# Two convolution layers on one core: x1's stores, the first small maps, layer 1's constants and the inner convolution rearranged

## The chip, the cores and the metric

The kernel runs on one core of a Trainium2 chip, in float32 throughout. The core has five engines that work through their own instruction lists in order and wait for each other through semaphores: TensorE (PE in the profile, with PEld for its weight loads), VectorE (DVE), ScalarE (ACT), GpSimd (POOL) and SyncE (SP), which here only issues DMA transfers. ScalarE issues transfers too. The metric is the device time of one execution in microseconds, lower is better.

## The reference

Input x is (8, 256, 64, 64). Two layers, each added to its own input, each preceded by a group normalisation `_gn` over 32 groups of 8 channels:

```python
# layer 0: an involution-like block; the 3x3 weights are computed from the input
x1 = conv1x1(x, w1, b1)                  # 32 channels
x2 = conv1x1(x, w2, b2)                  # 32 channels, unfolded 3x3 with reflect padding
x3 = conv1x1(x, w3, b3)                  # 256 channels, unfolded 3x3 with zero padding
h = relu(bn1(concat([x1, unfold3(x2)]))) # 320 channels
h = relu(bn2(conv1x1(h, cw1)))           # 32 channels: "the inner convolution"
w = conv1x1(h, cw2, cb2)                 # 32 groups x 9 taps
out = einsum("bgskhw,bgkhw->bgshw", unfold3(x3), w)
x = x + out
...
# layer 1: 7x7 local attention (4 heads of 64 channels) beside a dynamic 3x3 branch
att = softmax(einsum("bdn,bdkn->bnk", q, unfold7(k) + unfold7(pe)))
out_att = einsum("bnk,bdkn->bdn", att, unfold7(v))
wts = softmax(Wfc @ x, over the 9 taps)
out_conv = sum over taps of dwconv(relu(dwconv(x, w1)), w2) * wts
x = x + rate1 * out_att + rate2 * out_conv
```

## The kernel before

An image is cut into 8 bands of 8 rows (512 pixels), so there are 64 bands. One loop runs over g, from -12 to 63. In round g layer 1 works on band g, and layer 0 on the bands ahead of it: the small maps and value maps of band g + 12, the hidden maps of g + 11, the tap products of g + 10. Rounds -12 to -1 hold layer 0 alone (`alone`); from round 0 on both layers share the engines. From round 52 on layer 0 has nothing left.

A round has 8 steps, a step 6 positions. The order of each engine's instructions is written out by hand (`tc.manual_schedule()`): `beside` lists the work of a step at its head, middle and end, `steer` its loads, and `after(n, f)` puts f off by n positions. Calls of one position run in the order in which they were put off. The engines then wait only for data and for buffers: each tile has a tag with `bufs` slots, and a tile's writer waits for the readers of the tile that had its slot.

Layer 0 of one band, with the names that the change touches:

- `small_maps` (L332) makes x1 and x2 (64 channels) on TensorE, two half-bands of 4 rows stacked in one PSUM tile `small`. `write_maps` (L347, L351) adds the bias and writes them, three shifted copies of x2 and one of x1 for each half, eight ScalarE instructions. GpSimd then copies the edges (L357 to L366).
- `value_maps` (L375, L380, L382) makes x3 in two halves of 128 channels, `x3n`, and stores each to DRAM. In rounds of layer 0 alone ScalarE issues these stores. `values_by_group` (L396 to L404) reads them back in another layout, `x3q`.
- `hidden_maps` (L424) applies bn1 and relu in three instructions, `hid`, and TensorE does the inner convolution in 4 + 4 + 4 matmuls (L434). When layer 0 is alone all go to one PSUM tile and the second relu (L441) follows. Otherwise `one` does the first 8 in step 4 and ScalarE copies the sum out (L446); `two` does the last 4 in step 6, VectorE adds the copy (L450), and the relu follows.
- `tap_weights` makes the tap weights on TensorE (L470). VectorE multiplies each of the 9 with the shifted x3 (L483, `prod`, two slots). When layer 0 is alone TensorE sums three of the nine (L504) and VectorE adds that sum (L511, `combine`); all other products GpSimd adds to `xg`, which begins as x (L491). `take` reads the statistics for layer 1's normalisation (L519); `keep` then stores the finished x1 of the layer (`x<-xg`, four transfers, L529).

`x_tile` "xs" feeds the statistics of layer 0's normalisation some 9 bands ahead (`first_stats`, L287), and `scaled_weights` (L300, L301, L308) folds the normalisation into an image's weights; when the 8th band of an image's x1 is done, `norm_rows` computes layer 1's scale and bias. `load_rows`, `normalise` (L572), `values` (L601, L608) and `store_values` (L621, L625) then prepare layer 1's first bands.

The constants are loaded by `load`, all issued by ScalarE (L110). Those marked `now=False` (`c2`, the tap weights' matrix; `wq`, `wk`, `wv`, `wfc`, `mask` of layer 1) are put off and issued by `layer1_loads`, right before the first round. That also subtracts the ninth tap's column from `wfc` (`difference`, L205, two VectorE instructions), in rounds -10 and -9 of layer 0 alone, and scales `wv` (L200).

In layer 1, `branch_weights` (L886) is the largest matmul group, its exponentials go through ScalarE (L891), and `dynamic_sum` divides: GpSimd adds two sums (L899), limits the total (L902), VectorE takes reciprocals in two halves (L907), GpSimd multiplies (L908) and weighs the depthwise result `oc` (L912, L913), which ScalarE wrote in `depthwise_end` (L879). `oc` has two slots.

Of the kernel before, what the change touches and what calls it, by code (L numbers as in the profile page):

```python
# [10 lines left out]
F32 = mybir.dt.float32  # L11
# [7 lines left out]
P = 128  # L19
C = 256  # L20
# [67 lines left out]
def conv_layers_kernel(ctx: ExitStack, tc: tile.TileContext, ins: dict, out: bass.AP):  # L88
# [16 lines left out]

    late = []

    def load(name, shape, src=None, now=True):
        t = const.tile(shape, F32, name=f"c_{name}")
        late.append(lambda: nc.scalar.dma_start(out=t, in_=ins[name] if src is None else src))  # L110
        if now:
            late.pop()()
        return t
# [10 lines left out]
    gc = load("gc", [P, NCT, P])  # L124
    c2 = load("c2", [P, KK, P], now=False)
    wq = load("wq", [P, NCT, C], ins["wq"].rearrange("(t p) n -> p t n", p=P), now=False)
    wk = load("wk", [P, NCT, C], ins["wk"].rearrange("(t p) n -> p t n", p=P), now=False)
    wv = load("wv", [P, NCT, C], ins["wv"].rearrange("(t p) n -> p t n", p=P), now=False)
    wfc_in = ins["wfc"].rearrange("(t p) k n -> p t k n", p=P)
    wfc = load("wfc", [P, NCT, KK - 1, C], wfc_in[:, :, : KK - 1], now=False)  # L130

# [59 lines left out]
    def layer1_loads():  # L191


        last = w1.tile([P, NCT, 1, C], F32, tag="oc", name="last")
        for f in late:
            f()
        nc.scalar.dma_start(out=last, in_=wfc_in[:, :, KK - 1 :])

        def first():
            nc.vector.tensor_scalar(wv, wv, rate1, None, ALU.mult)  # L200

        def difference(kt):
            nc.vector.tensor_sub(wfc[:, kt], wfc[:, kt], last[:, kt].to_broadcast([P, KK - 1, C]))  # L205

        return [first, lambda: difference(0), lambda: difference(1)]

# [131 lines left out]
    def write_maps(b, i, p12, half):  # L340
        im = images[b]
        t, bias = im.x2[i], im.bias
        for u in half:
            r, o = u * R // 2, 64 * u
            for q, (dst, src) in enumerate(((1, 0), (0, 0), (0, 1))):
                n = W - (q != 1)
                nc.scalar.activation(  # L347
                    t[32 * q : 32 * q + 32, r + 1 : r + 1 + R // 2, dst : dst + n],
                    p12[o : o + 32, :, src : src + n], AF.Identity, bias=bias[o : o + 32, 0:1],
                )  # L350
            nc.scalar.activation(  # L351
                t[96:128, r : r + R // 2, :], p12[o + 32 : o + 64], AF.Identity, bias=bias[o + 32 : o + 64, 0:1]
            )
        if half[-1] == 0:
# [58 lines left out]
    def hidden_maps(b, i, alone):  # L413
# [7 lines left out]
        def hidden(t):  # L421
            n = P if t == 0 else 96
            hid = w0.tile([P, R, W], F32, tag="hid", name=f"hid_{b}_{i}_{t}", bufs=2)
            nc.scalar.activation(  # L424
                hid[:n], im.x2[i][:n, t : t + R, :], AF.Relu, bias=bn1b[:n, t : t + 1], scale=bn1s[:n, t : t + 1]
            )
            hids.append(hid)
# [14 lines left out]

        def one(home):
            ph = conv(home, 0, 2, 0, 1)
            after(1, lambda: hidden(2))
            after(2, lambda: nc.scalar.copy(h2, ph))  # L446

        def two(home):
            ph = conv(home, 2, 3, 2, 2)
            after(1, lambda: nc.vector.tensor_add(h2, ph, h2))  # L450
            after(3, lambda: relu(h2))

        hidden(0)
        after(3 if alone else 5, lambda: hidden(1))
        if alone:
# [4 lines left out]
            after(12, lambda: after(4, lambda ph=conv(home, 2, 3, 0, 2): relu(ph)))  # L460
        return [two, one]

    def tap_weights(b, i, u, alone, at):
# [49 lines left out]
        def take():  # L513
# [7 lines left out]
            if alone:  # L521
                after(9, lambda: keep(nc.scalar))
            else:
                keep(nc.sync)

        def keep(queue):
            for q in range(NQR):
                v = im.xg[i][q * REL : (q + 1) * REL].rearrange("p s r c -> p s (r c)")
                queue.dma_start(out=pieces(im.x1[i], q), in_=v)  # L529
# [346 lines left out]
    def depthwise_end(b, i, ct, acc):  # L876

        oc = w1.tile([P, BAND], F32, tag="oc", name=f"oc_{b}_{i}_{ct}")
        nc.scalar.activation(oc, acc.rearrange("p r c -> p (r c)"), AF.Copy, scale=rate2)  # L879
# [13 lines left out]
    def dynamic_sum(b, i, ct, ex, oc):  # L893
# [7 lines left out]

        engine.tensor_scalar(tot, tot, 1.0, 1.0e37, ALU.add, ALU.min)  # L902
        rec = w1.tile([P, BAND // 2], F32, tag="rec", name=f"rec_{b}_{i}_{ct}", bufs=1)
# [17 lines left out]

        after(9, lambda: quotient(0))
        after(13, lambda: quotient(1))
        after(15, weigh)


    def beside(g, s):
# [73 lines left out]
    def steer(g, s):  # L1001
# [22 lines left out]
    with tc.manual_schedule():  # L1024
# [15 lines left out]
        for _ in range(32):  # L1040
            advance()
        for n, f in enumerate(layer1_loads()):
            after(4 * STEPS * (3 + n), f)

        pending, before, conv, convs, maps = [], None, None, [], []
        for g in range(-AHEAD, B * NB):
            b, i = divmod(g, NB)
            for s in range(STEPS):
# [5 lines left out]
                if g >= 0:  # L1054
                    nm = f"{b}_{i}_{ct}_{m}"
                    weighted = []
                    if m % 2 == 0:
# [154 lines left out]
```

## Time and profile before

| what | value |
| --- | --- |
| time, median of 3 runs | 3856.01 us (3853.47 to 3856.48) |
| the profiled execution's own time | 3854.63 us |
| its span | 3852.8 us |
| mean granted TensorE clock | 0.994 |
| busy: PE / DVE / POOL / ACT | 97% / 89% / 81% / 73% |
| DMA | 490.14 MB, mean 127 GB/s |
| first matmul of `branch_weights` (L886) | at 235.5 us |

The profile is one execution. Its page gives the busy time of each engine, the span in 40 slices, the chain of work that ended last, and the costliest groups of instructions. The trace behind it answers finer questions: what an engine did in order of time in some stretch, and for what it waited. In an answer in order of time a line gives the start, the duration, the engine (SPq and ACTq are transfers being issued), the line of the kernel, the operation, its output and inputs, and in brackets how long the engine had been idle and who released it.

### The profile page before, as it was taken

The numbers are of one execution on the slowest core, as the hardware profiler recorded it, in microseconds if no ns is written. First come the engines' busy times: TensorE is split into PE (matmuls) and PEld (weight loads), VectorE is DVE, ScalarE is ACT, GpSimd is POOL, SyncE is SP. The second block draws the span as 40 slices with busy tenths as digits, with TensorE's granted clock in tenths as the row PEclk, the third lists the DMA queues.
The fourth block names the chain that finished last, engine by engine and source line by source line (L and its number), as shares of the span: only waits on it lengthen the run. The fifth ranks groups of instructions, "written<-read, shape, count | busy, mean of one in ns | idle before, by whom it ended". The sixth has DMA issues, their size and how long they took to land.

```text
span 3852.8 us, 71646 instructions
## 1 busy us (share of the span) xinstructions
PE 3756.3 (97%) x24620; PEld 2109.9 (55%) x24620; DVE 3434.4 (89%) x7125; ACT 2809.2 (73%) x6770; POOL 3116.8 (81%) x2100
## 2 busy tenths in 40 slices
PE   6889999999999999999999999999999999999998
PEld 3445555555555555555555555555555555555554
DVE  6879999999999999899998999999999899978877
ACT  4457777777777777777777777777777777677776
POOL 4868888888897888888888888888888888855565
PEclk9999999999999999999999999999999999999999
DMA  8764544544444544544544544454544544232221
GB/s 247 210 177 128 142 118 129 151 126 118 133 135 131 145 123 115 148 135 127 136 116 142 142 125 120 126 149 125 136 115 117 138 119 114 74 97 78 79 67 37
DMA packets 438926, 490.14 MB, mean 127 GB/s; under 512 B 62016, under 2 KB 324256, under 8 KB 438304
## 3 DMA queue, kind: packets, MB, share of 16 engines
q1 hardware_dynamic: 421984, 469.79, 44.1%
q10 hardware_dynamic: 16576, 15.76, 1.3%
q8 instruction: 194, 3.18, 0.4%
q14 instruction: 172, 1.41, 0.1%
HBM read 343.76 MB, written 145.10 MB: 127 GB/s over the span
## 4 chain that ended last, share of the span: by engine, by line
PE 81%; POOL 10%; DVE 3%; DMA 2%; ACT 2%; issue 2%; SPq 1%; ACTq 0%; POOLq 0%; DVEq 0%
PE pf L886 39%; PE small L799 6%; PE ptp L787 6%; POOL xg L491 6%; PE pk L706 5%; PE pq L684 5%; PE sco L750 5%; PE p L375 5%; PE pv L601 5%; PE pw L470 2%; POOL ex L1106 2%; PE small L332 1%; DVE prod L483 1%; PE small L434 1%; DMA x<-x3n 1%
## 5 line engine op out<-in xcount | busy, mean ns | idle before, releaser
L886 PE MATMUL pf<-yp,c_wfc 128*128 128x512 f32 x4096 | 1916.8, 594 | 11.3 <-DVE prod L483 6.3
L491 POOL TENSOR_TENSOR xg<-xg,prod 128x1024 f32<-128x1024 f32 x549 | 1199.8, 2185 | 132.5 <-DVE prod L483 103.6
L886 PEld LDWEIGHTS pf<-yp,c_wfc 128*128 128x128 f32 x4096 | 739.6, 190 | 711.4 <-issue 654.7
L1106 POOL TENSOR_TENSOR ex<-ex,ex 128x1024 f32<-128x1024 f32 x384 | 908.8, 2367 | 68.5 <-ACT ex L891 65.0
L891 ACT ACTIVATE ex<-pf 128x512 f32<-128x512 f32 x1024 | 604.0, 590 | 347.9 <-PE pf L886 269.2
L843 DVE SCALAR_TENSOR_TENSOR acc<-yp,c_chan,acc 128x504 f32<-128x504 f32 (+3 forms) x1104 | 775.5, 702 | 63.2 <-ACT acc L834 42.8
L483 DVE SCALAR_TENSOR_TENSOR prod<-pw,c_par,x3q 128x1040 f32<-128x1040 f32 x576 | 732.7, 1294 | 107.9 <-PE pw L470 60.8
L869 DVE SCALAR_TENSOR_TENSOR acc<-hid,c_chan,acc 128x504 f32<-128x504 f32 (+3 forms) x1024 | 751.1, 733 | 18.1
L781 ACT ACTIVATE prob<-prob,tot 128x196 f32<-128x196 f32 x1024 | 412.9, 452 | 242.4 <-DVE tot L779 236.8
L772 ACT ACTIVATE prob<-prob,nmax 128x196 f32<-128x196 f32 x1024 | 458.2, 450 | 101.3 <-DVE nmax L764 101.2
L907 DVE RECIPROCAL rec<-tot 128x256 f32<-128x256 f32 x256 | 445.7, 1741 | 28.3 <-POOL tot L902 27.5
L789 ACT COPY pt<-ptp 112x512 f32<-112x512 f32 x511 | 295.9, 579 | 111.8 <-PE ptp L787 111.8
L764 DVE CUSTOM_DVE_ANT_0 prob<-sco,c_mask 128x196 f32<-128x196 f32 x1024 | 324.8, 355 | 31.0 <-PE sco L750 31.0
L787 PEld LDWEIGHTS ptp<-ident,prob 128*112 128x112 f32 x2044 | 227.3, 133 | 184.4 <-issue 132.7
L787 PE MATMUL ptp<-ident,prob 128*112 128x128 f32 x2044 | 319.5, 279 | 0.0
L908 POOL TENSOR_TENSOR tot<-tot,rec 128x256 f32<-128x256 f32 x254 | 185.8, 732 | 145.7 <-DVE rec L907 139.7
L799 PEld LDWEIGHTS small<-pt,vt 112*64 112x64 f32 x8144 | 258.6, 138 | 79.8 <-issue 60.5
L799 PE MATMUL small<-pt,vt 112*64 112x64 f32 x8144 | 294.2, 225 | 3.3 <-DMA vt<-vd 1.8
L601 PE MATMUL pv<-c_wv,yp 128*128 128x256 f32 x1056 | 253.5, 383 | 1.8 <-ACT yp L572 1.8
L902 POOL TENSOR_SCALAR tot<-tot 128x512 f32<-128x512 f32 x127 | 243.9, 1920 | 11.1
L470 PEld LDWEIGHTS pw<-h2n,c_c 128*128 128x128 f32 x1152 | 175.1, 191 | 139.9 <-issue 115.9
L375 PE MATMUL p<-xc,w3s 128*128 128x512 f32 x512 | 243.3, 598 | 0.0
(136 smaller groups left out, 4656.7 us busy)
## 6 DMA issues: line engine op xcount, KB each, us to landing
vt<-vd SPq DMA_DIRECT2D x512, 112.0 KB
x3q<-x SPq DMA_DIRECT2D x128, 264.0 KB
xc<-in_x SPq DMA_DIRECT2D x64, 512.0 KB
xg<-in_xg SPq DMA_DIRECT2D x64, 512.0 KB
yp<-x SPq DMA_DIRECT2D x128, 256.0 KB
xr<-x SPq DMA_DIRECT2D x64, 512.0 KB
out_x<-xr SPq DMA_DIRECT2D x64, 512.0 KB
xs<-in_x SPq DMA_DIRECT2D x57, 512.0 KB
```

What stands on the lines that cost most here:

```text
L483: nc.vector.scalar_tensor_tensor(prod[:, :, :RUN], pw[:, j, :RUN].unsqueeze(1).to_broadcast([P, SHARE, RUN]), par[:, PCB2 + k : PCB2 + k + 1],
L491: nc.gpsimd.tensor_add(im.xg[i], im.xg[i], rows(prod))
L601: nc.tensor.matmul(pv[:, g], yp[:, kt, r : r + 2].rearrange("p r c -> p (r c)"), wv[:, kt], start=(kt == 0), stop=(kt == NCT - 1),)
L772: nc.scalar.activation(prob[:, h, :NKEY], prob[:, h, :NKEY], AF.Exp, bias=nmax[:, h : h + 1], scale=-1.0, accum_out=tot[:, h : h + 1],)
L787: nc.tensor.transpose(ptp[:, h, ch], prob[:, h, ch * CHUNK : (ch + 1) * CHUNK], ident)
L799: nc.tensor.matmul(po[half[h], :, t * TQ : (t + 1) * TQ], im.vt[i + ch, m][:n, t, (2 * ct + h) * HD : (2 * ct + h + 1) * HD], pt[:n, h, ch ...
L843: nc.vector.scalar_tensor_tensor(o, yp[:, ct, ra + dr : rb + dr, ca + dc : cb + dc], chan[:, ct, CW1 + k : CW1 + k + 1], o, ALU.mult, ALU.add,
L869: nc.vector.scalar_tensor_tensor(o, hid[:, ra + dr : rb + dr, ca + dc : cb + dc], chan[:, ct, CW2 + k : CW2 + k + 1], o, ALU.mult, ALU.add,)
L886: nc.tensor.matmul(pf, wfc[:, kt, 2 * m + j, ct * P : (ct + 1) * P], images[b].yp[i][:, kt, PAD : PAD + R], start=(kt == 0), stop=(kt == N ...
L891: nc.scalar.activation(ex[:, j].rearrange("p (r c) -> p r c", r=R), pf, AF.Exp)
L907: nc.vector.reciprocal(rec, v)
L1106: after(4, lambda ex=ex, exb=exb: nc.gpsimd.tensor_add(ex, ex, exb))
```

## The change

Layer 0 alone and layer 1's constants:

- `keep` issues two of x1's four stores by ScalarE and two by SyncE in rounds of layer 0 alone (before: four by ScalarE).
- In the first two bands VectorE writes the second half-band of the small maps; the value maps move to step 1, the statistics' load to step 6.
- `c2` is loaded with the first constants. Layer 1's constants are issued by SyncE, spread over the rounds: at position 48 n - 9 from the first round on, n from 2 to 7, `wfc` in four pieces. The scaling of `wv` moves to n = 5, the two differences to n = 8 and 9.

Both stages:

- `hid` has three slots (before two), `oc` one (before two). The third hidden map comes 14 positions after the first; beside layer 1 the inner convolution is one group of 12 matmuls in step 6, with the relu straight from PSUM; the copy and the add go.
- In `dynamic_sum`, for the first half of an image's last band, the limit comes 5 positions later, the first quotient 2, the second quotient and `weigh` 1.

```diff
+        else:
+            late[name] = lambda: nc.sync.dma_start(out=t, in_=ins[name] if src is None else src)
...
-    c2 = load("c2", [P, KK, P], now=False)
+    c2 = load("c2", [P, KK, P])
...
-    wfc = load("wfc", [P, NCT, KK - 1, C], wfc_in[:, :, : KK - 1], now=False)
+    wfc = const.tile([P, NCT, KK - 1, C], F32, name="c_wfc")
...
-        last = w1.tile([P, NCT, 1, C], F32, tag="oc", name="last")
-        for f in late:
-            f()
-        nc.scalar.dma_start(out=last, in_=wfc_in[:, :, KK - 1 :])
+        last = w1.tile([P, NCT, 1, C], F32, tag="oc", name="last", bufs=1)
+
+        def piece(n):
+            kt, k = n // 2, slice(n % 2 * (KK // 2), (n % 2 + 1) * (KK // 2))
+            nc.sync.dma_start(out=wfc[:, kt, k], in_=wfc_in[:, kt, k])
...
-        return [first, lambda: difference(0), lambda: difference(1)]
+        return [
+            (2, late["wq"]), (2, late["wk"]), (3, late["wv"]), (3, late["mask"]),
+            (4, lambda: piece(0)), (5, lambda: piece(1)), (6, lambda: piece(2)), (7, lambda: piece(3)),
+            (6, lambda: nc.sync.dma_start(out=last, in_=wfc_in[:, :, KK - 1 :])),
+            (5, scaled), (8, lambda: difference(0)), (9, lambda: difference(1)),
+        ]
...
+            def put(to, v, o, n):
+                if u and b == 0 and i < 2:
+                    nc.vector.tensor_scalar(to, v, bias[o : o + n, 0:1], None, ALU.add)
+                else:
+                    nc.scalar.activation(to, v, AF.Identity, bias=bias[o : o + n, 0:1])
...
-            hid = w0.tile([P, R, W], F32, tag="hid", name=f"hid_{b}_{i}_{t}", bufs=2)
+            hid = w0.tile([P, R, W], F32, tag="hid", name=f"hid_{b}_{i}_{t}", bufs=3)
...
-        def one(home):
-            ph = conv(home, 0, 2, 0, 1)
-            after(1, lambda: hidden(2))
-            after(2, lambda: nc.scalar.copy(h2, ph))
-
-        def two(home):
-            ph = conv(home, 2, 3, 2, 2)
-            after(1, lambda: nc.vector.tensor_add(h2, ph, h2))
-            after(3, lambda: relu(h2))
+        def inner(home):
+            ph = conv(home, 0, 3, 0, 2)
+            after(1, lambda: relu(ph))
...
-        return [two, one]
+        else:
+            after(14, lambda: hidden(2))
+        return [inner]
...
-                after(9, lambda: keep(nc.scalar))
+                after(9, lambda: keep((nc.scalar, nc.scalar, nc.sync, nc.sync)))
...
-        oc = w1.tile([P, BAND], F32, tag="oc", name=f"oc_{b}_{i}_{ct}")
+        oc = w1.tile([P, BAND], F32, tag="oc", name=f"oc_{b}_{i}_{ct}", bufs=1)
...
-        engine.tensor_scalar(tot, tot, 1.0, 1.0e37, ALU.add, ALU.min)
+        def limit():
+            engine.tensor_scalar(tot, tot, 1.0, 1.0e37, ALU.add, ALU.min)
+
+        late = 2 if (i, ct) == (NB - 1, 0) else 0
+        if late:
+            after(5, limit)
+        else:
+            limit()
...
-        after(9, lambda: quotient(0))
-        after(13, lambda: quotient(1))
-        after(15, weigh)
+        after(9 + late, lambda: quotient(0))
+        after(13 + late // 2, lambda: quotient(1))
+        after(15 + late // 2, weigh)
...
-            if s == (2 if alone else 0):
+            first = g < 2 - AHEAD
+            if s == (1 if first else 2 if alone else 0):
                 (mid if alone else end).append(lambda: value_maps(bq_, iq, 0, alone))
-            if s == (3 if alone else 1):
+            if s == (1 if first else 3 if alone else 1):
...
-        if s == (3 if g < -1 else 7) and g + AHEAD0 < B * NB:
+        if s == (6 if g < 2 - AHEAD else 3 if g < -1 else 7) and g + AHEAD0 < B * NB:
...
-        for n, f in enumerate(layer1_loads()):
-            after(4 * STEPS * (3 + n), f)
+        for n, f in layer1_loads():
+            after(6 * STEPS * n - 9, f)
...
-                        if s in (4, 6) and convs:
+                        if s == 6 and convs:
                             convs.pop()(small)
```

More of the change, by code (lines that the diff above doesn't have):

```diff
@@ L103, in load_x @@
         return t
-    late = []
+    late = {}
     def load(name, shape, src=None, now=True):
         t = const.tile(shape, F32, name=f"c_{name}")
-        late.append(lambda: nc.scalar.dma_start(out=t, in_=ins[name] if src is None else src))
         if now:
-            late.pop()()
+            nc.scalar.dma_start(out=t, in_=ins[name] if src is None else src)
+        else:
+            late[name] = lambda: nc.sync.dma_start(out=t, in_=ins[name] if src is None else src)
         return t
@@ L191, in layer1_loads, with scaled @@
     def layer1_loads():
-        last = w1.tile([P, NCT, 1, C], F32, tag="oc", name="last")
-        for f in late:
-            f()
-        nc.scalar.dma_start(out=last, in_=wfc_in[:, :, KK - 1 :])
-        def first():
+        last = w1.tile([P, NCT, 1, C], F32, tag="oc", name="last", bufs=1)
+        def piece(n):
+            kt, k = n // 2, slice(n % 2 * (KK // 2), (n % 2 + 1) * (KK // 2))
+            nc.sync.dma_start(out=wfc[:, kt, k], in_=wfc_in[:, kt, k])
+        def scaled():
             nc.vector.tensor_scalar(wv, wv, rate1, None, ALU.mult)
@@ L344, in write_maps @@
             r, o = u * R // 2, 64 * u
+            def put(to, v, o, n):
[3 more added lines that the diff above has]
+                    nc.scalar.activation(to, v, AF.Identity, bias=bias[o : o + n, 0:1])
             for q, (dst, src) in enumerate(((1, 0), (0, 0), (0, 1))):
                 n = W - (q != 1)
-                nc.scalar.activation(
+                put(
                     t[32 * q : 32 * q + 32, r + 1 : r + 1 + R // 2, dst : dst + n],
-                    p12[o : o + 32, :, src : src + n], AF.Identity, bias=bias[o : o + 32, 0:1],
+                    p12[o : o + 32, :, src : src + n], o, 32,
                 )
-            nc.scalar.activation(
-                t[96:128, r : r + R // 2, :], p12[o + 32 : o + 64], AF.Identity, bias=bias[o + 32 : o + 64, 0:1]
-            )
+            put(t[96:128, r : r + R // 2, :], p12[o + 32 : o + 64], o + 32, 32)
         if half[-1] == 0:
@@ L521, in take, with keep @@
             if alone:
-                after(9, lambda: keep(nc.scalar))
+                after(9, lambda: keep((nc.scalar, nc.scalar, nc.sync, nc.sync)))
             else:
-                keep(nc.sync)
-        def keep(queue):
-            for q in range(NQR):
+                keep((nc.sync,) * NQR)
+        def keep(queues):
+            for q, queue in enumerate(queues):
                 v = im.xg[i][q * REL : (q + 1) * REL].rearrange("p s r c -> p s (r c)")
```

## The prediction

> **What bounds the kernel now.** I read the page's busy shares first, then the busy time of each engine by stretches of time.
>
> ```profile
> span 3852.8 us, 71646 instructions
> PE 3756.3 (97%) x24620; PEld 2109.9 (55%) x24620; DVE 3434.4 (89%) x7125; ACT 2809.2 (73%) x6770; POOL 3116.8 (81%) x2100
> ...
> 20.00:40.00 20.00, 15.73 (x52) 8.30 (x52) 3.66 (x16) 11.49 (x26) 1.88 (x8) 1.00 0.86 302
> 100.00:120.00 20.00, 17.30 (x78) 8.06 (x77) 17.64 (x18) 9.70 (x19) 17.23 (x17) 0.91 0.73 200
> 240.00:260.00 20.00, 14.83 (x69) 7.80 (x68) 10.78 (x22) 11.65 (x26) 6.30 (x7) 0.83 0.65 203
> 800.00:1263.00 463.00, 460.65 (x3069) 261.08 (x3068) 426.33 (x890) 351.09 (x849) 396.80 (x265) 1.00 0.48 131
> ```
>
> (Columns: PE, PEld, DVE, ACT, POOL busy, PE's clock, DMA share, GB/s.) From about 256 us on TensorE is never free: an image of both layers takes 463 us and TensorE lacks 2.4 of them. So time is won in two places only: before 256 us, where the end moves with the moment TensorE fills up, and in those rare gaps. In layer 0 alone three things follow each other: a fill with VectorE idle (to 48.65 us, the first product), a steady part, and the entry to layer 1. VectorE and GpSimd in order of time, and the waits of the steady part:
>
> ```profile
> 48.65 3.72 DVE L483 SCALAR_TENSOR_TENSOR prod<-pw,c_par,x3q 128x1040 f32<-128x1040 f32 x3 [5.79 <-PE pw L470]
> 55.60 4.20 DVE L205 TENSOR_TENSOR c_wfc<-c_wfc,last 128x2048 f32<-128x2048 f32 x1
> 71.55 2.28 DVE L205 TENSOR_TENSOR c_wfc<-c_wfc,last 128x2048 f32<-128x2048 f32 x1
> 102.80 1.23 DVE L511 TENSOR_TENSOR xg<-sco_sum,xg 128x1024 f32<-128x1024 f32 x1 [0.66 <-POOL xg L491]
> 113.08 3.72 DVE L483 SCALAR_TENSOR_TENSOR prod<-pw,c_par,x3q 128x1040 f32<-128x1040 f32 x3 [1.67 <-PE pw L470]
> ...
> 107.90 11.24 POOL L491 TENSOR_TENSOR xg<-xg,prod 128x1024 f32<-128x1024 f32 x5 [2.14 <-DVE prod L483]
> ```
>
> The combines L511 mark the bands: 67.89, 86.45, 102.80, 119.17, 135.62, 157.49, 174.43, 191.15, 210.52 us. A plain band takes 16.35 us whether VectorE waits for GpSimd (0.95 + 0.66 near 100 us) or for TensorE (1.67 at 113): a ring of VectorE and GpSimd sets it. GpSimd: six adds of 2.18 = 13.1, edge copies 0.8, wait 2.14, sum 16.0. That wait is VectorE's combine, statistics and two products (1.23 + 1.29 + 2.4) less GpSimd's copies and one add (3.0). None of these changes.
>
> ScalarE and SyncE where transfers delay them:
>
> ```profile
> 139.96 5.09 ACTq L529 DMA_DIRECT2D x<-xg  x4
> 145.16 0.81 ACT L424 ACTIVATE hid<-x,bn1b,bn1s 96x512 f32<-96x512 f32 x1 [5.65 <-DMA x<-xg]
> ...
> 219.39 1.96 ACTq L529 DMA_DIRECT2D x<-xg  x3
> 222.18 0.35 ACT L608 COPY vc<-pv 128x256 f32<-128x256 f32 x1
> ...
> 222.55 1.30 SPq L621 DMA_DIRECT2D vd<-vc  x2
> ```
>
> And the largest gap of TensorE with both layers, once in each of images 0 to 5 (6.3 us in all), here in image 2:
>
> ```profile
> 1609.02 1.75 DVE L907 RECIPROCAL rec<-tot 128x256 f32<-128x256 f32 x1 [0.95 <-POOL tot L902]
> 1611.28 1.30 DVE L483 SCALAR_TENSOR_TENSOR prod<-pw,c_par,x3q 128x1040 f32<-128x1040 f32 x1 [0.51 <-POOL xg L491]
> 1612.64 1.98 PE L886 MATMUL pf<-yp,c_wfc 128*128 128x512 f32 x4 [1.04 <-DVE prod L483]
> ```
>
> **What the Trainium skill says.** "DMA: Bandwidth & Descriptors", section "Issuing engines are not separate DMA queues": a second issuing engine saves only sequencer time. The trace agrees on that time: 0.63 us for one x1 store on ScalarE. "TensorE: Matmul & The Clock Gate", "What's actually happening": an idle TensorE falls to half its clock. It shows: L504's four matmuls take 3.65 us at 106.69, 1.88 at 112.83; the fill's value maps run at 0.69 us each, not 0.43. "Perfetto Trace Analysis", "Optimization Strategy": the same bubble repeating can mean a lack of buffers; the 1.04 us gap is such a one, a PSUM slot that `prod` frees late.
>
> **The change part by part.**
>
> *c2 early.* 576 KB join a stretch whose DMA runs at 370 to 400 GB/s: 1.5 us. VectorE takes the statistics there with 0.4 us idle, so all of it is late: +1.5 (bounds 0 to 2.2, the latter at the mean 272 GB/s of the first 20 us).
>
> *Fill.* TensorE sets the fill first: value maps of band 0 end at 33.5, + 1.5 = 35.0; then small maps 1.0 and value maps 3.7 of band 1 end at 39.7. ScalarE's half of the maps (4 x 0.47 = 1.9) is hidden under the value maps; VectorE's half costs four of about 0.48 us (estimate from L714, PSUM source: 0.75 for 512 columns, 0.42 for 192), on an idle engine, its next statistics moved behind it. Then x3n 0.7, its store 0.35, three hidden maps 2.3, the last convolution and cold small maps 2.6, tap weights 1.4: first product at 47.7 instead of 48.65. **-1.0.** Before, ScalarE also waited 1.1 us at 42 us to issue a store under the traffic of the constants; that goes with them.
>
> *Differences moved.* At 55.6 us L205 holds the products to 59.7; without it they start when the tap weights end, 57.2: -2.45. At 71.55 the whole 2.2 falls out (band 0 to 1 takes 18.56, a plain band 16.35). At rounds 8 and 9 the two come back with 2.2 each, but into waits: behind the biases near 149 us (VectorE then still waits 1.28 + 0.43 for GpSimd) and before a 1.75 wait for TensorE at 166 us. I take 0.5 each (0 to 2.2). **-3.65.**
>
> *Constants by SyncE.* Nine issues of about 0.45 us in a queue with gaps of 4 to 7 us a band, 3.2 MB into a DMA 75% busy there, over six bands: +14%, hidden. If not, 3.2 MB at 220 GB/s are 15 us.
>
> *x1's stores.* 18 of 36 issues leave ScalarE, 1.25 us a band. In plain bands the ring hides that. SyncE's two stand behind xs (100.96) and must wait for the combine (104.0); queued behind them are xg, used 14 us later, and the first x3q piece; the other x3q pieces wait until 108.7 anyway for x3n's stores. Nothing is late. Two places feel it: at 140 us the normalisation of image 1 stands behind 5.09 us of issues, VectorE waiting 2.41 for it; half is 2.5, of which I take 1.0, since GpSimd's waits follow (0 to 2.5). In the entry `vc` (222.18) stands behind the stores, SyncE waits for it and from 222.55 to 260 us issues without a pause: 2 x 0.63 = 1.3. **-2.3.** SyncE is idle from 208 to 222, so its two stores cost nothing.
>
> *hid's third slot.* TensorE waits 14.4 us for `hid` over nine bands; the ring hides it: 0 (bound -8, under 1 us a band).
>
> *Inner convolution.* The same 12 matmuls; a copy of 0.25 (ScalarE) and an add of 0.28 (VectorE) go in 53 rounds. TensorE is the bound there, so 0; eight matmuls more in step 6 (0.44 us) delay VectorE's `add_values` on the same tile, the lost add repays 0.28.
>
> *Last band's limit.* The limit now comes after one xg add on GpSimd: one add from 1607.0 to 1609.2, the limit (1.92) to 1611.1. VectorE does the product at 1609.3, not behind the reciprocal at 1611.28; the slot is free at 1610.6, a microsecond before TensorE asks. The reciprocal follows at about 1611.9, its limit done. **-6.2** (six images; bounds -6.3 and 0). A stall may reappear at the reciprocal, where the margin is 0.8 us.
>
> *oc with one slot.* ScalarE's write must wait for GpSimd's last read (L913). Over the 127 pairs in the trace GpSimd is done 0.71 us or more ahead, 1.15 to 1.76 in most second halves: 0.
>
> Sum: -1.0 - 3.65 - 2.3 - 6.2 = -13.2 on the profiled execution's 3854.6 (its span of 3852.8 and 1.8 around it). The runs' median is 1.4 higher: 3856.0 - 13.2 = 3842.8.
>
> **The rivals.** *Only one half comes:* the 7 us of the start get lost in other waits of the ring or the DMA, or the gap reappears: 3849.5. For it: the ring swallowed other waits too. *More comes:* with hid and ScalarE freed, plain bands lose about 1 us each over eight: 3835. For it, 14.4 us of TensorE's waits and VectorE's 1.67; against it, bands without that wait are no shorter. *Slower: oc's single slot binds.* If GpSimd ends its weighing later, relative to ScalarE, by more than 0.7 to 1.8 us, ScalarE stops, and behind it stand the exponentials that free TensorE's PSUM. At 0.5 us in each of 53 second halves: 3842.8 + 26 = 3869. It decides once GpSimd slips by those margins; against it, GpSimd's list changes only in the last bands, where the margins are 3.0 and 4.5.
>
> **How the numbers follow.** Forecast 0.61 (own range 3837 to 3848), half 0.15, more 0.12, slower 0.12. No change means within 0.2%, 7.7 us, about what a measurement of this kernel can tell: 3848.3 to 3863.7. Faster 0.61 + 0.12 = 0.73, same 0.15, slower 0.12. The range goes from 3833 (more, with its spread) to 3858 (half, with constants not hidden); outside lie most of the slower case and some 0.06 of tails.
>
> **What would show it.** First product near 47.7 and combine of band 1 near 81 us (before 86.45); plain bands still 16.3; first L886 some 7 us earlier than 235.5; no 1 us gap ahead of L886 in band 7 of each image; GpSimd ahead of each oc write. Wrong: statistics not late for c2, x3q or xg arriving after their products, plain bands shorter, or new TensorE gaps beside layer 1.

## The result and the profile after

| | before | after |
| --- | --- | --- |
| time, median of 7 runs each | 3854.44 us (3849.93 to 3858.00) | 3867.58 us (3862.30 to 3871.63) |
| ratio | | 1.0033 (95%: 1.0022 to 1.0043) |
| profiled execution, its own time | 3854.63 us | 3865.45 us |
| its span | 3852.8 us | 3863.6 us |

The kernel became 13 us slower; 13 us faster was forecast. The lines of the code have moved by a few: `branch_weights`, whose PSUM tile is `pf` in the lines, is now L892, its exponentials L897, GpSimd's sum of two taps L1120, the adds to `xg` L497, `prod` L489, the combine L517, the limit L909, the inner convolution L444.

First the page's head and the busy time by stretches of the changed kernel (PE, PEld, DVE, ACT, POOL busy, the share of full clock that TensorE was granted, DMA share, GB/s):

```profile
span 3863.6 us, 71661 instructions
PE 3760.9 (97%) x24620; PEld 2112.5 (55%) x24620; DVE 3427.3 (89%) x7080; ACT 2801.3 (73%) x6709; POOL 3118.2 (81%) x2100
...
20.00:40.00 20.00, 14.54 (x52) 7.93 (x52) 8.40 (x25) 7.56 (x17) 1.72 (x8) 1.00 0.34 110
100.00:120.00 20.00, 15.67 (x79) 7.66 (x77) 16.86 (x16) 10.32 (x18) 15.73 (x16) 1.00 0.93 260
240.00:260.00 20.00, 16.31 (x72) 8.74 (x71) 12.09 (x28) 14.43 (x33) 7.41 (x7) 0.83 0.74 226
800.00:1263.85 463.85, 460.41 (x3066) 260.86 (x3064) 423.92 (x881) 349.59 (x839) 396.16 (x264) 1.00 0.49 131
```

The busy shares are as good as unchanged, and TensorE is still at 97%. What moved are two things. The traffic of the constants left the fill (DMA share 0.34 between 20 and 40 us, 0.86 before) and came back around 100 us (0.93, 0.73 before). And an image with both layers takes 463.8 us where it took 462.4.

The span's +10.8 us can be read off three marks, the first `oc` write (L885; before L879) of each image and the last one:

| | before | after | difference |
| --- | --- | --- | --- |
| first `oc` write of image 0 | 269.7 | 268.2 | -1.5 |
| from there to that of image 6, six images | 2774.4 | 2782.7 | +8.3 |
| from image 6 to image 7 (layer 0 has no more to do) | 429.9 | 430.9 | +1.0 |
| image 7, from its first to its last `oc` write | 364.0 | 365.8 | +1.8 |
| from the last write to the end | 14.8 | 16.0 | +1.3 |

So the start won 1.5 of the forecast 7 us, each image lost 1.4 instead of winning 1.0, and the end lost 3.

**The start.** VectorE in layer 0 alone, in order of time:

```profile
48.79 3.72 DVE L489 SCALAR_TENSOR_TENSOR prod<-pw,c_par,x3q 128x1040 f32<-128x1040 f32 x3 [8.08 <-DMA x3q<-x]
...
66.19 1.30 DVE L489 SCALAR_TENSOR_TENSOR prod<-pw,c_par,x3q 128x1040 f32<-128x1040 f32 x1 [3.42 <-DMA x3q<-x]
83.76 1.23 DVE L517 TENSOR_TENSOR xg<-sco_sum,xg 128x1024 f32<-128x1024 f32 x1 [0.54 <-POOL xg L497]
99.76 1.30 DVE L489 SCALAR_TENSOR_TENSOR prod<-pw,c_par,x3q 128x1040 f32<-128x1040 f32 x1 [1.34 <-DMA x3q<-x]
117.61 1.30 DVE L489 SCALAR_TENSOR_TENSOR prod<-pw,c_par,x3q 128x1040 f32<-128x1040 f32 x1 [2.16 <-DMA c_wfc<-in_wfc]
```

Before, the first product waited for TensorE's tap weights; now it waits for the load of `x3q` and starts at the same moment (48.65, 48.79). The two differences are gone from bands 0 and 1 as forecast: the second combine stands at 83.76, 2.7 us earlier than the 86.45 of before. But VectorE now waits four more times for DMA, which it did nowhere before in its products (three are shown, the fourth is 0.42 us at 174.63). The combines then stand at 101.0, 118.8, 136.9 us (before 102.8, 119.2, 135.6): these bands take 17.2 to 18.1 us, not 16.35, and the lead is lost. The last of the lines names `c_wfc` as what ended its wait, a constant that the product does not read; releasers are inferred, and what was late is presumably the last `x3q` piece, which SyncE issued 0.7 us ahead of that piece of `c_wfc` (113.30 and 114.02).

SyncE's own queue shows what else is late in the same place:

```profile
85.01 4.99 SPq L535 DMA_DIRECT2D x<-xg  x2
90.09 0.56 SPq L421 DMA_DIRECT2D xg<-in_xg  x1
90.70 0.57 SPq L406 DMA_DIRECT2D x3q<-x  x1
...
102.22 4.53 SPq L535 DMA_DIRECT2D x<-xg  x2
...
122.42 1.24 SPq L535 DMA_DIRECT2D x<-xg  x2
```

Two stores of x1 take SyncE 1.24 us where the issue goes through at once, and 4.99 and 4.53 us in two of the bands in which constants are loaded (the last piece of a constant was issued 9 and 7 us earlier; after the pieces at 114 us they take 1.24 again). The next `x3q` loads stand behind them. The first `pf` starts at 235.2 us (235.5 before).

**Both layers.** The gap that the later limit was to close, image 2, band 7, TensorE, VectorE and GpSimd in order of time:

```profile
1610.72 2.18 POOL L497 TENSOR_TENSOR xg<-xg,prod 128x1024 f32<-128x1024 f32 x1
1612.94 1.30 DVE L489 SCALAR_TENSOR_TENSOR prod<-pw,c_par,x3q 128x1040 f32<-128x1040 f32 x1 [1.68 <-POOL xg L497]
1612.99 1.92 POOL L909 TENSOR_SCALAR tot<-tot 128x512 f32<-128x512 f32 x1
1615.45 1.88 PE L892 MATMUL pf<-yp,c_wfc 128*128 128x512 f32 x4
1615.63 1.74 DVE L920 RECIPROCAL rec<-tot 128x256 f32<-128x256 f32 x1
```

The step went as forecast: one add to `xg`, then the limit, the product ahead of the reciprocal, and `pf` without a wait. But elsewhere TensorE has new waits. Its waits between 300 and 3800 us, by what was waited for; the kernel after, then the kernel before:

```profile
PE pf L892 <- ACT ex L897: 15.6, 37, 1.0
```

```profile
PE pf L886 <- DVE prod L483: 6.3, 6, 1.1
PE pf L886 <- ACT ex L891: 4.4, 10, 1.1
```

(Total, number, longest.) One kind of wait went, 6.3 us in six; another grew from 4.4 to 15.6. Where it stands: TensorE, GpSimd and ScalarE in steps 5 and 6 of an inner band (image 2, band 2), after, in order of time engine by engine:

```profile
1319.62 1.89 PE L607 MATMUL pv<-c_wv,yp 128*128 128x256 f32 x8
1321.85 1.99 PE L892 MATMUL pf<-yp,c_wfc 128*128 128x512 f32 x4 [0.34 <-ACT ex L897]
...
1325.92 0.86 PE L444 MATMUL small<-hid,c_c 128*32 128x128 f32 x24
...
1314.38 4.46 POOL L497 TENSOR_TENSOR xg<-xg,prod 128x1024 f32<-128x1024 f32 x2
1318.79 2.37 POOL L1120 TENSOR_TENSOR ex<-ex,ex 128x1024 f32<-128x1024 f32 x1
1321.24 1.27 POOL L905 TENSOR_TENSOR tot<-ex 128x512 f32<-128x512 f32 x1
...
1321.20 0.60 ACT L897 ACTIVATE ex<-pf 128x512 f32<-128x512 f32 x1 [2.51 <-POOL ex L1120]
```

and the same place before:

```profile
1309.26 0.65 PE L434 MATMUL small<-hid,c_c 128*32 128x128 f32 x16
...
1319.81 1.89 PE L886 MATMUL pf<-yp,c_wfc 128*128 128x512 f32 x4
...
1323.79 0.43 PE L434 MATMUL small<-hid,c_c 96*32 96x128 f32 x8
...
1319.07 0.60 ACT L891 ACTIVATE ex<-pf 128x512 f32<-128x512 f32 x1 [1.91 <-POOL ex L1106]
```

GpSimd runs without a pause here; its sum releases ScalarE's exponential, and that frees the PSUM slot of the next `pf`. Before, 16 matmuls of the inner convolution in step 4 occupied TensorE while GpSimd got there, and ScalarE alone waited (1.91 us). After, TensorE arrives early, ScalarE waits 2.51 us and TensorE 0.34; and the work taken out of step 4 is then done in step 6, behind the wait.

Summed over one whole image (the third), each matmul group counted from its start to the next one's, without the gap between them: the inner convolution itself costs 6.37 us, not 7.47, as one group of 24 needs less than 16 and 8 (the trace has two records for each of the 12 matmuls in the code); but gaps ahead of `pf` are 2.43, not 1.50, although the gap of band 7 has gone, and the groups of `pv` take 29.56, not 28.53, with the same matmuls (presumably short waits inside them). The chain of work that ended last shows it as well, after and before:

```profile
PE 61%; POOL 23%; DVE 6%; ACT 3%; issue 3%; DMA 2%; SPq 0%; ACTq 0%; POOLq 0%; DVEq 0%
```

```profile
PE 81%; POOL 10%; DVE 3%; DMA 2%; ACT 2%; issue 2%; SPq 1%; ACTq 0%; POOLq 0%; DVEq 0%
```

GpSimd carries twice as much of the path, although its busy time is the same.

**The end.** GpSimd in image 7's last band, after and then before:

```profile
3844.12 0.73 POOL L921 TENSOR_TENSOR tot<-tot,rec 128x256 f32<-128x256 f32 x1 [3.87 <-DVE rec L920]
...
3847.52 4.76 POOL L1120 TENSOR_TENSOR ex<-ex,ex 128x1024 f32<-128x1024 f32 x2
```

```profile
3833.39 0.73 POOL L908 TENSOR_TENSOR tot<-tot,rec 128x256 f32<-128x256 f32 x1 [2.14 <-DVE rec L907]
...
3836.78 4.79 POOL L1106 TENSOR_TENSOR ex<-ex,ex 128x1024 f32<-128x1024 f32 x2
```

In the last image there is no layer 0 left to fill GpSimd: it waits for the later quotient, and the sums that everything after it needs stand behind. They start 10.7 us later than before, where the last image's first `oc` write is 7.8 later: the 3 us of the end.

### The profile page after: what moved, and what is told of

It is laid out like the page before. It is cut to its first block, busy times and chain, and to the rows that moved or that the text cites. A ratio compares the mean times of both kernels' runs of the same rounds, so it can differ in the third digit from the quotient of the medians.

```text
span 3863.6 us, 71661 instructions
## 1 busy us (share of the span) xinstructions
PE 3760.9 (97%) x24620; PEld 2112.5 (55%) x24620; DVE 3427.3 (89%) x7080; ACT 2801.3 (73%) x6709; POOL 3118.2 (81%) x2100
## 4 chain that ended last, share of the span: by engine, by line
PE 61%; POOL 23%; DVE 6%; ACT 3%; issue 3%; DMA 2%; SPq 0%; ACTq 0%; POOLq 0%; DVEq 0%
PE pf L892 30%; POOL xg L497 13%; POOL ex L1120 7%; PE small L805 5%; PE p L385 5%; PE sco L756 4%; PE ptp L793 4%; PE pq L690 3%; PE pk L712 3%; DVE prod L489 2%; PE pv L607 2%; POOL oc L925 1%; PE small L337 1%; PE pw L476 1%; PE small L444 1%
## 5 line engine op out<-in xcount | busy, mean ns | idle before, releaser
L892 PE MATMUL pf<-yp,c_wfc 128*128 128x512 f32 x4096 | 1920.1, 595 | 16.7 <-ACT ex L897 15.6
L497 POOL TENSOR_TENSOR xg<-xg,prod 128x1024 f32<-128x1024 f32 x549 | 1201.4, 2188 | 135.1 <-DVE prod L489 105.8
L892 PEld LDWEIGHTS pf<-yp,c_wfc 128*128 128x128 f32 x4096 | 739.2, 190 | 725.3 <-issue 659.5
L1120 POOL TENSOR_TENSOR ex<-ex,ex 128x1024 f32<-128x1024 f32 x384 | 908.3, 2365 | 59.4 <-ACT ex L897 55.4
L897 ACT ACTIVATE ex<-pf 128x512 f32<-128x512 f32 x1024 | 605.5, 591 | 387.9 <-PE pf L892 282.1
L489 DVE SCALAR_TENSOR_TENSOR prod<-pw,c_par,x3q 128x1040 f32<-128x1040 f32 x576 | 732.6, 1294 | 108.7 <-PE pw L476 47.7
L875 DVE SCALAR_TENSOR_TENSOR acc<-hid,c_chan,acc 128x504 f32<-128x504 f32 (+3 forms) x1024 | 750.6, 733 | 18.1
L355 ACT ACTIVATE x<-small,bias 32x252 f32<-32x252 f32 x504 | 233.2, 463 | 45.4 <-PE small L337 38.3
L909 POOL TENSOR_SCALAR tot<-tot 128x512 f32<-128x512 f32 x127 | 243.9, 1920 | 11.1
```

The lines of the kernel that those rows point to most:

```text
L489: nc.vector.scalar_tensor_tensor(prod[:, :, :RUN], pw[:, j, :RUN].unsqueeze(1).to_broadcast([P, SHARE, RUN]), par[:, PCB2 + k : PCB2 + k + 1],
L497: nc.gpsimd.tensor_add(im.xg[i], im.xg[i], rows(prod))
L875: nc.vector.scalar_tensor_tensor(o, hid[:, ra + dr : rb + dr, ca + dc : cb + dc], chan[:, ct, CW2 + k : CW2 + k + 1], o, ALU.mult, ALU.add,)
L892: nc.tensor.matmul(pf, wfc[:, kt, 2 * m + j, ct * P : (ct + 1) * P], images[b].yp[i][:, kt, PAD : PAD + R], start=(kt == 0), stop=(kt == N ...
L897: nc.scalar.activation(ex[:, j].rearrange("p (r c) -> p r c", r=R), pf, AF.Exp)
L1120: after(4, lambda ex=ex, exb=exb: nc.gpsimd.tensor_add(ex, ex, exb))
```

## The experiments

All ratios are to the kernel before, run beside on the same chip. There were three sets of runs on three chips, in which its medians were 3854.03, 3853.95 and 3853.79 us. A profile is one execution, and executions of one kernel spread over 2 to 13 us. The period of an image repeats to 0.4 us from image to image and from kernel to kernel with the same code, so its differences are read from the traces; those of the start are judged by the medians.

### The inner convolution in one piece, alone

Done on the kernel before; the third `hid` slot and the single `oc` slot are what it needs.

```diff
-        def one(home):
...
-        def two(home):
...
+        def inner(home):
+            ph = conv(home, 0, 3, 0, 2)
+            after(1, lambda: relu(ph))
...
-        return [two, one]
+        else:
+            after(14, lambda: hidden(2))
+        return [inner]
...
-                        if s in (4, 6) and convs:
+                        if s == 6 and convs:
```

> The kernel before with only the inner convolution in one piece in step 6 (three hid slots and, for the room, one oc slot). Theory P (place): the eight matmuls stood in step 4 ahead of a point where TensorE has to wait for GpSimd's sums anyway; moved behind it they lengthen TensorE's round by 0.42 us. Then this kernel alone is 14 to 18 us slower than before (about 3870). Rival O (oc's single slot makes ScalarE wait): also slower, but with waits of ScalarE's oc for GpSimd. Rival S (the loss comes from layer 0 alone, constants and stores): no change, within 2 us.

Measured: 3866.24 us, ratio 1.0033 (1.0020 to 1.0046). An image takes 464.9 us, 2.5 more than before. This part by itself makes nearly the loss of the whole change, a little less than the 14 to 18 us expected. Its profile has the new waits too: TensorE waits 15.4 us in 37 waits for ScalarE's exponential ahead of `pf`, against 4.4 in ten before.

### The later limit, alone

```diff
+        late = 2 if (i, ct) == (NB - 1, 0) else 0
+        if late:
+            after(5, limit)
+        else:
+            limit()
...
-        after(9, lambda: quotient(0))
+        after(9 + late, lambda: quotient(0))
```

(the second quotient and `weigh` as in the change.)

> The kernel before with only the later limit and quotients in each image's last band. The 1.04 us gap in six images goes (-6.5), and in the last image the later weighing delays the final sums by some 3 us: 3.5 us faster in all (about 3851). If the tail is not its doing: 6 us faster. If the gap is not its doing: 3 us slower.

Measured: 3849.55 us, ratio 0.9988 (0.9981 to 0.9994). An image takes 461.1 us, 1.3 less, a little more than the gap's 1.04. From image 7's first `oc` write to the end it takes 3.0 us more (365.6 + 16.2 against 364.0 + 14.8). So -7.8 + 3.0 = -4.8 by the trace, -4.5 by the medians.

### The change with the convolution in two pieces again

```diff
-        def inner(home):
...
+        def one(home):
...
+        def two(home):
...
-                        if s == 6 and convs:
+                        if s in (4, 6) and convs:
```

> The changed kernel with the inner convolution in two pieces again, in steps 4 and 6, all else changed. Theory P: the whole 16 us of the convolution come back, some 5 us faster than before (about 3849). Rival O: no better than the changed kernel, since oc still has one slot. Rival S: no better than the changed kernel, about 13 us slower than before.

Measured: 3850.78 us, ratio 0.9991 (0.9983 to 0.9999), 461.1 us an image: the period of the later limit alone. `oc` still has one slot here, and TensorE's waits for ScalarE are what they were before:

```profile
PE pf L896 <- ACT ex L901: 4.4, 10, 1.1
```

So neither the single slot nor the start makes the loss; the convolution does.

### The change with the convolution in one piece, but in step 4

The same matmuls, ahead of the wait for GpSimd and not behind it; the third hidden map comes four positions earlier for that.

```diff
-            after(14, lambda: hidden(2))
+            after(10, lambda: hidden(2))
...
-                        if s == 6 and convs:
+                        if s == 4 and convs:
```

> The changed kernel with the inner convolution in one piece, but in step 4 (the third hidden map 10 positions after the first, so that it is there). Theory P: as good as the two pieces, within 2 us (about 3849), because the twelve matmuls lie ahead of the wait. If one piece as such costs (its length on one PSUM tile, the copy and add were free): about 3865, as the changed kernel.

Measured: 3842.19 us, ratio 0.9968 (0.9956 to 0.9980), 460.0 us an image. That is 7 us better than expected. The same work at another place: 3.8 us an image, 25 us in all, lie between steps 4 and 6. The third hidden map moved as well, but the changed kernel has no wait of TensorE for `hid` between 300 and 3800 us. TensorE in the same band:

```profile
1307.89 0.87 PE L444 MATMUL small<-hid,c_c 128*32 128x128 f32 x24
...
1318.67 1.88 PE L892 MATMUL pf<-yp,c_wfc 128*128 128x512 f32 x4
```

No gap ahead of `pf`, though ScalarE's exponential still waits 1.67 us for GpSimd's sum. GpSimd's share of the chain that ended last is 5% here and 6% in the version in two pieces, 24% with the convolution alone in step 6. The 1.1 us an image that it wins on the version in two pieces is the inner convolution's saving in TensorE's time (7.47 us an image there, 6.37 here).

### And without the later limit in the last two images

```diff
-        late = 2 if (i, ct) == (NB - 1, 0) else 0
+        late = 2 if (i, ct) == (NB - 1, 0) and b < B - 2 else 0
```

> The changed kernel with the convolution in one piece in step 4 and the later limit left out in the last two images, where no gap stands. If the later limit lengthens the tail: 3 us faster than with it in all images (about 3839.5, against 3842.2). If not: 3842. Layer 0 alone is as in the changed kernel; first oc near 268 to 273 us.

Measured: 3837.16 us, ratio 0.9959 (0.9946 to 0.9971): 5.0 us less than with it, 3.0 by the traces. The end's loss is the later limit's. This and the next kernels beat both the kernel before and the change.

### What the parts of layer 0 alone bring

Four kernels, each the last one with parts of layer 0 alone undone. Constants as before:

```diff
-        for n, f in layer1_loads():
-            after(6 * STEPS * n - 9, f)
+        for n, f in enumerate(layer1_loads()):
+            after(4 * STEPS * (3 + n), f)
```

(and `load`, `c2`, `wfc` and `layer1_loads` as before.)

> The one before, with the constants loaded as in the kernel before (all by ScalarE ahead of the first round, c2 too; the differences early). Theory K: the constants spread over the rounds by SyncE make the taps' x3 arrive late; then first oc is 6 to 8 us earlier, near 263 us, and the time about 3832. Theory Q (x1's stores by SyncE hold up its queue): 0 to 2 us faster only.

x1's stores all by ScalarE:

```diff
-                after(9, lambda: keep((nc.scalar, nc.scalar, nc.sync, nc.sync)))
+                after(9, lambda: keep((nc.scalar,) * NQR))
```

> The first of this set, with all four of x1's stores by ScalarE again. Theory Q: first oc 6 to 8 us earlier and the time about 3832. Theory K: 0 to 2 us faster, or 1 to 2 slower since ScalarE's issues come back ahead of the third hidden map.

Constants, stores and the first bands all as before (`put` by ScalarE alone, value maps in steps 2 and 3, statistics' load in step 3); the third `hid` slot stays:

```diff
-                if u and b == 0 and i < 2:
+                if False:
...
-            if s == (1 if first else 2 if alone else 0):
+            if s == (2 if alone else 0):
```

> The first of this set, with layer 0 alone as before in all but the third hid slot: constants, x1's stores, first bands as before. Both theories: first oc near 262 us, as with the convolution in step 6 alone, so 8 us faster than the first of the set (about 3831). If the earlier start of that run was chance: first oc near 269, about 3839.

Constants and stores as before, the first bands as in the change (both edits above):

> The convolution in step 4, the later limit without the last two images, three hidden slots, and of the parts in layer 0 alone only that of the first bands (VectorE takes half of their small maps, value maps one step earlier); constants and x1's stores as before. Without that part as well the time was 3836.1. The prediction's step for the fill is -1.0 with 1.5 us for c2, which is loaded late here, so -2.5: 3833.6. If the fill is set by x3q's arrival instead (VectorE's first product waits for it): 3836, no difference.

| constants | x1's stores | first bands | median, us | ratio |
| --- | --- | --- | --- | --- |
| spread, SyncE | half by SyncE | changed | 3837.16 | 0.9959 (0.9946 to 0.9971) |
| as before | half by SyncE | changed | 3836.76 | 0.9955 (0.9941 to 0.9968) |
| spread, SyncE | all by ScalarE | changed | 3846.65 | 0.9982 (0.9974 to 0.9989) |
| as before | all by ScalarE | changed | 3836.52 | 0.9956 (0.9943 to 0.9970) |
| as before | all by ScalarE | as before | 3836.10 | 0.9955 (0.9942 to 0.9967) |

All have 460.0 us an image; they differ in the start alone. With the constants as before, sharing the stores is worth nothing. With the constants spread, it is worth 9.5 us, and just brings the kernel back to where it was without either. Taking the constants out of the fill, sharing the stores and rearranging the first bands together bring nothing. Neither theory that one of the two edits costs 5 us by itself holds, and the kernel with all three as before, for which 3831 was expected, is no faster than the first. The third and the fourth of these kernels, both with all four stores by ScalarE, in the same band, engine by engine; constants spread, then as before. The last line of each covers the stretch from 84 to 146 us (columns as above; the granted clock is the third figure from the end):

```profile
90.60 4.63 ACTq L535 DMA_DIRECT2D x<-xg  x4
95.28 0.81 ACT L434 ACTIVATE hid<-x,bn1b,bn1s 96x512 f32<-96x512 f32 x1 [5.13 <-DMA x<-xg]
96.15 0.65 PE L444 MATMUL ph<-hid,c_c 96*32 96x128 f32 x8 [3.58 <-ACT hid L434]
96.73 1.69 PE L476 MATMUL pw<-h2n,c_c 128*128 128x132 f32 x6
84.00:146.00 62.00, 50.97 (x229) 25.52 (x227) 51.76 (x54) 28.05 (x52) 46.60 (x37) 0.89 0.83 234
```

```profile
88.64 3.60 ACTq L530 DMA_DIRECT2D x<-xg  x4
92.29 0.81 ACT L429 ACTIVATE hid<-x,bn1b,bn1s 96x512 f32<-96x512 f32 x1 [4.10 <-DMA x<-xg]
93.15 0.42 PE L439 MATMUL ph<-hid,c_c 96*32 96x128 f32 x8 [1.24 <-ACT hid L429]
93.51 0.94 PE L471 MATMUL pw<-h2n,c_c 128*128 128x132 f32 x6
84.00:146.00 62.00, 47.94 (x269) 23.96 (x267) 54.81 (x61) 28.55 (x54) 50.22 (x39) 1.00 0.86 233
```

The hidden maps stand behind the stores, and TensorE's convolution behind those. With the constants spread, TensorE comes to wait 3.58 us here (4.22 in the next band), and the tap weights after it take 1.69 us instead of 0.94, at a lower granted clock (0.50 between 97 and 99 us). But slow stores are not what tells the two apart: from band 0 on four of them take ScalarE 4.98, 4.63, 4.52 and 2.59 us with the constants spread, 5.33, 3.60, 4.27 and 2.68 with the constants in the fill, and 2.69, 3.46, 3.12 and 3.02 in the kernel before. The first `pf` is at 242.4 and 231.1 us. How much of the 9.5 us is lateness and how much the clock was not separated.

### The third `hid` slot alone

```diff
-            hid = w0.tile([P, R, W], F32, tag="hid", name=f"hid_{b}_{i}_{t}", bufs=2)
+            hid = w0.tile([P, R, W], F32, tag="hid", name=f"hid_{b}_{i}_{t}", bufs=3)
```

(and one slot for `oc`.)

> The kernel before with three slots for the hidden map and, to make room, one slot for the scaled sums; nothing else. Theory H (the third slot is what shortens the start, about 3 us at the median: with the convolution in one piece in step 6 and nothing changed in layer 0 alone, the images' own +2.5 us x 6 and +0.9 for the last make +15.7, but +12.2 was measured): 3851, both layers' period as before, 462.4. Theory Z (the slot gives nothing, as predicted; the difference was spread from run to run): 3854.

Measured: 3853.04 us, ratio 0.9998 (0.9990 to 1.0006), 462.4 us an image. The slot gives nothing by itself. The first experiment's profile has its first `pf` at 228.7 us and this one at 235.7, with the same code up to there: the shorter start of the first was spread between executions.

### Only the parts in layer 0 alone

The change with two `hid` slots, the convolution in two pieces in steps 4 and 6 and the limit as before; `oc` with one slot.

> Only the parts of the change in layer 0 alone (constants spread over SyncE, half of x1's stores by SyncE, first bands' copies shared) and one slot for the scaled sums; two hidden slots, the convolution in two pieces and the limit in its old place. The prediction's sum for these parts is -7: 3847. Theory H (they give nothing together, their gains being eaten by loads that come late in the same stretch): 3854, give or take 2, and slower than with the third hidden slot alone.

Measured: 3859.68 us, ratio 1.0014 (1.0007 to 1.0020): 5.9 us slower, where the prediction's sum was 7 faster and the expectation nothing. 462.4 us an image, so all of it is in the start; the first `pf` comes at 240.4 us. VectorE and SyncE, in order of time:

```profile
66.59 1.30 DVE L493 SCALAR_TENSOR_TENSOR prod<-pw,c_par,x3q 128x1040 f32<-128x1040 f32 x1 [3.27 <-DMA x3q<-x]
139.37 1.30 DVE L493 SCALAR_TENSOR_TENSOR prod<-pw,c_par,x3q 128x1040 f32<-128x1040 f32 x1 [4.74 <-DMA x3q<-x]
...
87.03 5.91 SPq L539 DMA_DIRECT2D x<-xg  x2
105.05 3.63 SPq L539 DMA_DIRECT2D x<-xg  x2
```

The products wait for loads that were in time before, and SyncE stands in x1's stores. That these 5.9 us are about 1 in the comparison above (3837.16 against 3836.10) goes with the third `hid` slot there and the two here; how the slot covers for late loads stays open, and the three parts were not taken apart with two slots.

## Why the prediction was wrong

The three parts of the change, each alone on the kernel before, add up to the whole: +5.9 for the parts of layer 0 alone, +12.2 for the convolution in step 6 with its slots, -4.5 for the limit, +13.6; the whole change measured +13.1. That it closes to half a microsecond is in part luck: the first and the third together with a third `hid` slot, as the change has it, measured -3.3, not +1.4. From there the traces lead to the change without a sum of medians: with the convolution in step 6 instead of in two pieces, the six images take 16.1 us more and the step from image 6 to 7 takes 1.0 more.

- **Inner convolution: 0. This is the step that failed.** The prediction said "TensorE is the bound there, so 0". TensorE is busy 99.5% of an image (460.65 of 463 us before) and still not the bound in every step: around step 5 GpSimd is, with no pause between two adds, a sum and the next total, and TensorE had just enough other work to hide it. Putting the first of its matmuls (16 in the trace) into step 6 made the group there 0.43 us longer (0.79, not 0.36), and a band of the first experiment is 0.31 longer: taking them out of step 4, where they took 0.57, brought only 0.12 back. Place alone is worth 3.8 us an image. The opposite sign was hidden in the same edit: one group of 24 takes TensorE 0.79 us where 16 and 8 took 0.57 + 0.36, 1.1 us an image, which is what the version in step 4 collects. There the 0.22 us by which the group in step 4 grew are paid, and the 0.36 of step 6 saved: the wait hides about as much as stood ahead of it before, and no more.
- **Last band's limit: -6.2.** Mechanism right; its main term was a little small (-1.3 us an image, not -1.04). A term was missing: +3.0 in image 7, where layer 0's work does not hide the later weighing. Net -4.5.
- **Fill: -1.0.** The first product did not move (48.65, 48.79). TensorE was the limit of the fill before; `x3q`, loaded through SyncE, was close behind (VectorE waits 8.08 us for it after; with the third `hid` slot alone it is also `x3q` that the first product waits for, at 50.00). The working followed one engine's list and left this load out; the steps it lists also add up to 47.1, not to the 47.7 it names. Undone, it changes nothing (3836.5 and 3836.1).
- **Differences moved: -3.65.** They went from bands 0 and 1 as said, and the second combine came 2.7 us earlier; 81 had been forecast, 83.8 came. What followed ate it.
- **Constants by SyncE: 0, "hidden"; if not, 15.** They were not hidden. With all stores by ScalarE, spreading them cost 10.1 us (3846.65 against 3836.52), what `c2` and the moved differences do included, and with the stores shared 0.4 (3837.16 against 3836.76). The DMA share rose to 0.93 where 0.73 had been, but it was 0.88 there with the constants in the fill and the stores shared, so the share alone says little. The price came as lateness of others: VectorE's waits for `x3q` of up to 4.7 us, and up to 5.9 us for two stores to be issued. The bound of 15 was named and given too little weight.
- **x1's stores: -2.3.** "Nothing is late" was wrong: each profile with constants spread and stores shared that is shown here has SyncE in two stores for 4.5 us and more, with `x3q` queued behind. The edit is worth 0 with the constants as before and 9.5 with them spread, so it had no value of its own to be summed.
- **hid's third slot: 0.** Right by itself (0.9998). **oc with one slot: 0.** Right: in the whole trace ScalarE waits for GpSimd's reading of `oc` once, 0.2 us, in the very last band:

```profile
ACT oc L885 <- POOL xr L926: 0.2, 1, 0.2
```

The slower rival named 3869 us, close to the 3867.6 that came, but by `oc`'s single slot, which did not bind. The wait it named, ScalarE behind GpSimd with the exponentials that free TensorE's PSUM, is close to the one that does: it came through the order of TensorE's work, not through a buffer. The rival of half the gain and that of more fall with the measurement.

## What to carry to other kernels

An engine that is 99% busy over a period can still be led by another one in a part of it. Before moving work within the period, look at each step for what the others wait for there: work moved from ahead of such a wait to behind it is paid for the greater part (here 0.48 of 0.79 us a band), and work that stands ahead of it is free only as far as the wait reaches. And when transfers are spread out to hide them, count who else loads in that stretch, and which stores are issued there: the cost shows as the lateness of others and as time in the issuing engine, not in the moved transfers.

## What was not expected

Two stores of x1, 1.24 us to issue on SyncE, took 3.6 to 5.9 us in some of the bands in which constants were loaded, and never above 2.03 us in the one kernel that shares the stores and has the constants in the fill. Constants in flight are not the whole of it: with only the parts in layer 0 alone two stores took 4.02 us at 163.98, 30 us after the last constant was issued, and four by ScalarE took 5.09 us at 140 in the kernel before. The inner convolution's 24 matmuls took TensorE 0.79 us in one group, from its start to the next group's, and 0.57 + 0.36 in groups of 16 and 8. And one and the same start of a kernel varies: first `pf` at 235.2, 236.5, 237.9 and 237.3 us in four profiles whose code in layer 0 alone is the same, and at 228.7, 230.2 and 235.7 in three others (the convolution alone, layer 0 alone as before, the slot alone). The granted clock goes with it: between 45 and 235 us its mean is 0.93 to 0.95 in the four profiles that reach `pf` by 231.1 us, 0.89 to 0.93 in the nine that reach it at 233.5 or later, and 0.95 against 0.90 in the first and the last of those three. Whether the lower clock makes the later start, or the waits of a later start the lower clock, no run here tells apart.
